# Layer 0 of a two-layer graph network: from one hand-written order of the products to three streams that a program clock merges, with the first pair also done by seven products

## The chip, the cores and the metric

The kernel runs on one core of one Trainium2 chip, in one launch. A core has TensorE (PE, matrix products into PSUM), ScalarE (ACT), VectorE (DVE), GpSimd (POOL) and SyncE (SP, which issues DMAs); PSUM, where products land, has eight banks of 128 x 512 float32. Everything here is float32. The metric is the device time of the core in microseconds, the median over runs: 2367.74 us before, from runs of 2363.7 to 2368.15 us.

## The reference, cut to what matters

`x` is 64 matrices of 256 x 256, `adj` one matrix of 256 x 256. Both layers are residual and begin with a layernorm and a relu.

```
G = adj * adj
h = relu(layernorm(x))
x = x + G relu(G relu(G h W1) W2) W3        # layer 0: W1 256x512, W2 512x1024, W3 1024x256
h = relu(layernorm(x))
U = eigenvectors of the normalised Laplacian of adj      # 256 x 256
x = x + U (relu(U^T h V1 + b1) V2 + b2)     # layer 1: V1 256x128, V2 128x256
```

Layer 0 needs only `G`, so it can run while the eigenvectors are found. Layer 1 needs `U`, except for its product `h V1`, which the kernel takes first, because `U^T h V1` is `U^T (h V1)`.

## The kernel before, in words

**Two kinds of work.** The class `Eigen` finds the eigenvectors by tridiagonalising and joining: a long chain of small DVE, POOL and ACT instructions with a few products (tiles `psA` to `psD`), one after the other. The class `Layers` works on 32 pairs `q` of input matrices. For each pair of layer 0 there are, in order: `begin` (load, layernorm and relu into `h0`, on ACT and POOL), `first` (G times h0, tile `y1`), `widened` (times W1, with a relu into `s1`), the spread (G times `s1`), the products with W2, `fourth` (with W3, tile `p3`), `last` (G times `p3`, added to `x1` on DVE and stored), `norm1` (layernorm of the new rows on ACT and POOL), `turn_rows` (PE transposes) and `for_layer1` (times V1, tile `hw`, stored).

**By seven.** For pairs from `SEVEN_FROM` = 1 on, the W2 product is made of seven half-sized products in place of eight. That needs sums of blocks of W2 (`fold_weights`: eight DVE subtractions and additions of 128 x 512, six into the tile `sums` and two in place), sums of blocks of its right-hand side (`spread_by_seven`: `forms` 0 to 2 are copied from PSUM, `forms` 3 to 5 are a copy of the negated block `forms` 6, and one DMA from POOL adds 0 to 2 onto 3 to 5), and a sum at the end (`add`, twice a pair, once for each half `jj`: a POOL DMA adds three blocks from `parts` onto `s2`). After each `add`, `rectify` applies the relu on ACT, and `fourth` can read that half. Pair 0 goes by eight (`third`, with the tile `y2`).

**Who sets the order.** The program writes out PE's and ACT's instruction order itself. A clock in the program, the class `Pace` (line 160), estimates when each instruction could start. The eigen chain calls `chain`: before it hands out an instruction of its own, `run` hands out those instructions of the streams that start earlier by the clock's estimate. `run` looks only at the head of each stream. DVE, POOL and SP get their order from the framework (the `manual_schedule` in `tile_kernel` names PE and ACT only), but each engine executes its own queue strictly in order.

**Two streams.** `streams` (line 1902) makes two: `products` (line 1905), which holds all PE work of layer 0 with the ACT copies that empty its PSUM banks, in one fixed order, and `rows`, which holds both norms, `begin(q + 2)` ahead of `norm1(q)`. Pair by pair the order in `products` is:

```
W2 of q (with last(q-1) between its first products), first(q+1), widened(q+1),
rectify half 0, turn_rows(q-1), spread part 1 of q+1, rectify half 1,
fourth of q, part 1, for_layer1(q-1), load of x1,
then the other spread parts of q+1 in turn with the other parts of fourth of q
```

**PSUM.** Layer 0 has four banks. `bank` gives them out in rotation, except those that are `held` over several products. Layer 1 has four more.

**The end.** When the chain has U, `go_on` hands out another 3.5 us of PE work, a flag is read by every engine (`mend`), and layer 1 runs as a further stream. The last pair's `turn_rows` waits for `due`, which is set there.

## Time and profile before

| what | value |
|---|---|
| median of three runs | 2367.74 us |
| the profiled execution, its own time | 2369.36 us |
| its span, first to last instruction | 2367.6 us |
| PE busy | 2290.2 us (97%) |
| PE weight loads busy | 1854.7 us (78%) |
| DVE, ACT, POOL busy | 2005.0, 1183.8, 698.7 us |
| PE idle from 100 to 1300 us, and from 1300 to 2150 us | 23.9 us, 22.9 us |
| flag of the eigen chain written | 2173.8 us |
| first product of layer 1 | 2181.0 us |

In the profile a PE row's time covers a run of products of one kind; two records stand for one float32 product of 256 columns. A product's record lasts beyond the time at which the next can start, so the pace of a run is read from one row's start to the next row's start. `bank<-L_gnn_W,y` is `widened`, `bank<-gt,s` the spread, `bank<-forms,...` the W2 products, `bank<-L_gnn_W,s` the products with W3, `bank<-p,gt` is `last`, `bank<-eye,x` is `turn_rows`, `bank<-L_gnn_W,x` is `for_layer1`, and `bank<-hw,u` the first product of layer 1. In square brackets stands how long the engine sat idle just before, and what ended that. All instructions carry line 208, where `issue` calls them.

### The profile page before, as it was taken

The page shows a single profiled execution, that of the slowest core. Times are in us where ns is not written, and L with a number is a line of the kernel's source. Part 1 is how long each engine was busy: PE and PEld are TensorE (multiplying, and loading weights), DVE is VectorE, ACT ScalarE, POOL GpSimd, SP SyncE. Part 2 cuts the span into 40 slices and gives each one's busy share as a digit, 9 for nine tenths or more (in the row PEclk, how much of TensorE's full clock was granted, in tenths as well). Part 3 has the DMA queues.
Part 4 walks back from the last instruction along what each step waited for, and adds up shares of the span by engine and source line. Part 5 has one row for each costly group of instructions (what it writes and reads, how often), then busy time and mean ns, then how long its engine had stood idle before and what let it go on. Part 6 is the DMA issues. An engine that isn't in the chain of part 4 may idle for free. (4 is left out here: it accounts for less than half of the span.)

```text
span 2367.6 us, 40804 instructions
## 1 busy us (share of the span) xinstructions
PE 2290.2 (97%) x10652; PEld 1854.7 (78%) x10652; DVE 2005.0 (85%) x12072; ACT 1183.8 (50%) x2951; POOL 698.7 (30%) x1946
## 2 busy tenths in 40 slices
PE   7999999999999999999999899999999999999999
PEld 4687878787777877787888788777778777887888
DVE  7999999999999999999999899999877687882343
ACT  4455554555555555555555345555554455543322
POOL 3444544445554222222222001111111111111443
PEclk9999999999999999999999999999999999999999
DMA  4022222122222222222222222322322222223675
GB/s 134 23 70 61 65 57 70 51 69 63 59 59 62 72 56 61 69 67 59 72 63 60 58 63 72 72 72 59 72 63 63 59 58 72 54 63 103 217 251 203
DMA packets 91359, 183.26 MB, mean 77 GB/s; under 512 B 8432, under 2 KB 61808, under 8 KB 91120
## 3 DMA queue, kind: packets, MB, share of 16 engines
q0 software_dynamic: 13392, 73.14, 15.6%
q1 hardware_dynamic: 77728, 107.45, 13.4%
q8 instruction: 86, 1.41, 0.2%
q14 instruction: 153, 1.25, 0.2%
HBM read 65.48 MB, written 41.94 MB: 45 GB/s over the span
## 5 line engine op out<-in xcount | busy, mean ns | idle before, releaser
L208 PE MATMUL bank<-forms,L_gnn_W 128*128 128x256 f32 (+2 forms) x2102 | 490.7, 382 | 9.2 <-DVE x L208 6.1
L208 PE MATMUL bank<-L_gnn_W,s 128*128 128x256 f32 x2086 | 476.0, 378 | 4.8 <-ACT s L208 4.7
L208 PEld LDWEIGHTS bank<-forms,L_gnn_W 128*128 128x128 f32 x2102 | 390.6, 191 | 73.3 <-issue 11.7
L208 PEld LDWEIGHTS bank<-L_gnn_W,s 128*128 128x128 f32 x2086 | 391.7, 192 | 57.3 <-ACT s L208 5.7
L208 ACT ACTIVATE s<-bank 128x512 f32<-128x512 f32 (+1 forms) x485 | 278.7, 579 | 174.3 <-PE bank L208 173.3
L208 PE MATMUL bank<-forms,sums 128*128 128x256 f32 (+1 forms) x1512 | 347.0, 377 | 0.0
L208 PEld LDWEIGHTS bank<-forms,sums 128*128 128x128 f32 x1512 | 283.3, 191 | 53.4 <-issue 15.5
L208 PE MATMUL bank<-gt,s 128*128 128x256 f32 (+1 forms) x1036 | 246.3, 377 | 1.1 <-ACT s L208 1.1
L208 PE MATMUL bank<-L_gnn_W,y 128*128 128x512 f32 (+3 forms) x538 | 230.8, 572 | 1.1 <-ACT y L208 1.1
L208 ACT ACTIVATE forms<-bank 128x512 f32<-128x512 f32 x217 | 128.9, 594 | 180.9 <-PE bank L208 180.7
L208 PEld LDWEIGHTS bank<-gt,s 128*128 128x128 f32 x1036 | 188.9, 190 | 24.8 <-ACT s L208 2.6
L208 POOL COPY m<-xr 128x1 f32<-128x1 f32 x254 | 59.9, 236 | 418.1 <-DVE xr L208 418.0
L208 PEld LDWEIGHTS bank<-L_gnn_W,y 128*128 128x128 f32 x538 | 98.7, 190 | 98.2 <-issue 87.3
L208 ACT ACTIVATE junk<-xr 128x254 f32<-128x254 f32 (+63 forms) x127 | 46.0, 362 | 200.5 <-DVE xr L208 200.4
L208 ACT ACTIVATE junk<-x 128x256 f32<-128x256 f32 x256 | 105.8, 413 | 71.9 <-issue 44.0
L208 DVE SCALAR_TENSOR_TENSOR A<-xr,wc,A 128x255 f32<-128x255 f32 (+63 forms) x381 | 139.2, 368 | 0.0
L208 DVE SCALAR_TENSOR_TENSOR A<-wr,q,A 128x255 f32<-128x255 f32 (+63 forms) x381 | 138.0, 365 | 0.0
L208 ACT ACTIVATE junk<-x,nm 128x256 f32<-128x256 f32 x256 | 128.7, 503 | 4.0
L208 PE MATMUL bank<-p,gt 128*128 128x512 f32 (+2 forms) x272 | 122.8, 567 | 0.0
L208 PE MATMUL bank<-gt,h 128*128 128x256 f32 (+1 forms) x520 | 119.1, 379 | 0.1
L208 DVE SCALAR_TENSOR_TENSOR r<-A,xr 128x255 f32<-128x255 f32 (+63 forms) x381 | 117.8, 309 | 0.2
L208 PE MATMUL psB<-ident,ac 128*128 128x128 f32 x381 | 84.7, 277 | 27.2 <-DVE z L208 15.0
(614 smaller groups left out, 4639.5 us busy)
## 6 DMA issues: line engine op xcount, KB each, us to landing
x<-in_x_dram SPq DMA_DIRECT2D x128, 256.0 KB, 3.0
x<-x SPq DMA_DIRECT2D x64, 512.0 KB, 3.5
forms<-forms POOLq DMA_DIRECT2D x31, 768.0 KB, 5.8
s<-s POOLq DMA_DIRECT2D x31, 768.0 KB, 5.9
s<-forms POOLq DMA_DIRECT2D x31, 768.0 KB, 5.8
hw<-hw SPq DMA_DIRECT2D x64, 256.0 KB, 3.1
out_dram<-out SPq DMA_DIRECT2D x64, 256.0 KB, 2.2
L_gnn_W<-in_L_gnn_W_dram SPq DMA_DIRECT2D x1, 2048.0 KB, 11.2
```

What stands on the lines that cost most here:

```text
L208: return op.call(*op.args, **op.kwargs)
```

## The change

- `products` is replaced by three streams that the clock merges: `narrow` (first, widened and spread of the next pair), `wide` (fold_weights, W2, rectify, fourth, last) and `turned` (turn_rows, for_layer1, load of x1). What orders them against each other are sets that they fill: `added` opens `widened` once the first `add` of the pair before has been handed out, `tripled` opens the spread once all its W2 products have, `formed` opens the W2 products, and `loaded` opens `last`.
- `rows` is split into one stream for each norm. `due` is gone.
- All pairs go by seven; `third` by eight, `y2`, `first_pair`, `spread_of` and `spread_in_turn` are gone. `fold_weights` is the first thing in `wide`.
- The blocks that the second `add` reads are now `forms` 3 to 5 in place of 0 to 2, and the four spread blocks follow one another in one bank.
- The four banks are four fixed tiles. `take` waits in the program for one that has been given back, and picks the one that the clock says is free first.
- The clock keeps the source of a DMA as being read until the DMA lands (4 or 6 us in its estimate), and no longer only for the time of its issue.

```diff
@@ class Pace
+    def free_at(self, t):
+        name, _, _ = span(t)
+        return max((x[2] for x in (*self.written.get(name, ()), *self.read.get(name, ()))), default=0.0)
@@ issue
-            self.read[name] = [*self.read[name][-15:], (lo, hi, start + busy, engine)]
+            self.read[name] = [*self.read[name][-15:], (lo, hi, start + (until if "dma" in op.name else busy), engine)]
@@ class Layers
-        self.parts = [self.s1.rearrange("p m b f -> p (m b) f")[:, 1:4], forms[:, 0:3]]
+        self.parts = [self.s1.rearrange("p m b f -> p (m b) f")[:, 1:4], forms[:, 3:6]]
-        self.banks, self.held = list(range(4)), {}
+        self.free_banks = [self.ps.tile([P, 512], F32, name=f"bank{i}") for i in range(4)]
+    def take(self):
+        yield lambda: len(self.free_banks) > 0
+        ps = min(self.free_banks, key=self.pace.free_at)
+        self.free_banks = [x for x in self.free_banks if x is not ps]
         return ps
+    def give(self, ps):
+        self.free_banks.append(ps)
     def streams(self):
-        return Stream(self.products()), Stream(self.rows())
+        return [Stream(x) for x in (self.narrow(), self.turned(), self.wide(), self.rows(), self.new_rows())]
+    def narrow(self):
+        for q in range(PAIRS):
+            yield from self.first(q)
+            yield lambda: q == 0 or q - 1 in self.added
+            for b in range(2):
+                yield from self.widened(b)
+            yield lambda: q == 0 or q - 1 in self.tripled
+            yield from self.spread()
+            self.formed.add(q)
+    def wide(self):
+        yield from self.fold_weights()
+        for q in range(PAIRS):
+            last = self.last(q - 1) if q > 0 else iter(())
+            yield lambda: q in self.formed
+            for part in self.third(q):
+                if part is None:
+                    yield from next(last, ())
+                else:
+                    yield part
+            self.tripled.add(q)
+            yield from self.fourth()
+        for part in self.last(PAIRS - 1):
+            yield from part
+    def turned(self):
+        for q in range(PAIRS + 1):
+            if q > 0:
+                yield lambda: q - 1 in self.h1
+                yield from self.turn_rows()
+                yield from self.for_layer1(q - 1)
+            if q < PAIRS:
+                for i in range(2):
+                    yield self.nc.sync.dma_start(out=self.x1[:, i], in_=self.view(self.ap["x"], q)[:, i])
+                self.loaded.add(q)
@@ third (was third_by_seven)
         yield from part("z", 0, 4, 2)
         yield self.add(0)
+        self.added.add(q)
@@ fourth
+        for jj in range(2):
+            yield from self.rectify(jj)
             for m in range(H):
-                yield from part(m, 0, at)
+                yield from part(m, 0, range(4 * jj, 4 * jj + 4))
+        for m in range(H):
             yield from part(m, 1, range(8))
             yield self.nc.scalar.copy(self.p3[:, m, :], banks[m])
-            self.free(banks[m])
+            self.give(banks[m])
```

## The prediction

> **What bounds the kernel.** I read the page first, then PE's waits in two stretches, then PE's timeline at a wait, and last the stretch in which the eigen chain ends.
>
> ```profile
> PE 2290.2 (97%) x10652; PEld 1854.7 (78%) x10652; DVE 2005.0 (85%) x12072; ACT 1183.8 (50%) x2951; POOL 698.7 (30%) x1946
> ```
>
> PE is busy for 2290.2 of 2367.6 us. PE's timeline in the middle of a pair says whether that is real work:
>
> ```profile
> 1628.31 7.03 PE L208 MATMUL bank<-L_gnn_W,y 128*128 128x512 f32 x16
> 1635.17 1.04 PE L208 MATMUL bank<-eye,x 128*128 128x128 f32 x8
> 1636.05 1.89 PE L208 MATMUL bank<-gt,s 128*128 128x256 f32 x8
> ```
>
> Start to start, 16 records of 512 columns take 6.86 us (0.429 each) and 8 of 256 take 1.73 (0.216 each), without a hole. So PE bounds the kernel, and all that another order can win is PE's idle time, 77.4 us. Of this 11.8 us (two waits, 4.6 and 7.2) are the start, where no product can run yet. The next answers, PE's waits from 100 to 1300 us and from 1300 to 2150 us, give most of the rest.
>
> ```profile
> PE psB L208 <- DVE z L208: 13.2, 17, 1.9
> PE psB L208 <- DVE xr L208: 9.0, 11, 1.7
> PE psB L208 <- DVE ac L208: 1.2, 2, 1.0
> ...
> PE bank L208 <- DVE x L208: 6.1, 5, 3.6
> PE bank L208 <- ACT s L208: 4.7, 2, 3.8
> ...
> PE bank L208 <- ACT forms L208: 3.2, 3, 1.1
> PE bank L208 <- ACT x L208: 1.3, 1, 1.3
> ```
>
> In the first stretch (23.4 us) PE waits only in front of the chain's transposes `psB`. That looks like the chain's fault, but the timeline of PE, and of ACT beside it, shows what lies ahead of such a wait:
>
> ```profile
> 766.90 1.04 PE L208 MATMUL bank<-eye,x 128*128 128x128 f32 x8
> 769.67 0.29 PE L208 MATMUL psB<-ident,ac 128*128 128x128 f32 x1 [1.73 <-DVE xr L208]
> ...
> 769.91 1.89 PE L208 MATMUL bank<-gt,s 128*128 128x256 f32 x8
> ...
> 769.23 1.56 ACT L208 ACTIVATE s<-s 128x1024 f32<-128x1024 f32 x2
> 770.70 0.57 ACT L208 COPY x<-bank 128x512 f32<-128x512 f32 x1
> ```
>
> The spread product at 769.91 needs only `s1`, which was ready, yet it stands behind `psB`. In the single stream it follows the ACT work of `rectify` and `turn_rows`, which a busy ACT reaches only at 769.23. The head of the stream waited for ACT, so the clock had no PE work to put ahead of `psB`. About one wait a pair is of this kind. Where PE had work the wait is shorter:
>
> ```profile
> 677.09 1.03 PE L208 MATMUL bank<-forms,L_gnn_W 128*128 128x256 f32 x4
> 678.78 0.40 PE L208 MATMUL psB<-ident,ac 128*128 128x128 f32 x2 [0.66 <-DVE z L208]
> ```
>
> The end of the chain, again PE's timeline: the last flag product of the chain is at 2173.26, and layer 0 still has 46 records with W3 and 8 of `last` after it, 9.9 + 3.4 us, then 2.6 us of transposes and V1 products. Layer 1 takes 165 us of PE after that.
>
> ```profile
> 2173.26 0.28 PE L208 MATMUL psC<-bad,ones 128*128 128x1 f32 x2
> 2173.40 4.56 PE L208 MATMUL bank<-L_gnn_W,s 128*128 128x256 f32 x20
> ...
> 2194.39 3.02 PE L208 MATMUL bank<-ut,s 128*128 128x256 f32 x8 [2.80 <-ACT s L208]
> ```
>
> **The change, part by part.** The sum is made against the profiled execution, 2369.36 us (span 2367.6 and 1.8 around it), which is 1.6 us above the median of the runs, 2367.74.
>
> *Pair 0 by seven.* Removed are 64 records of 512 columns, 64 x 0.429 = 27.5 us, and 16 short ACT copies. Added are 112 records of 256, 112 x 0.216 = 24.2, with 14 copies, two `rectify` (1.6 us each), one triple copy (1.48) and three POOL DMAs (issue 0.9 to 1.0 us each, 5.8 to landing) on queues that are idle there for most of the time. **-3.3 us.** The three DMAs lie behind the first six W2 products (10.3 us); without that cover each would cost its 5.8.
>
> *Three streams.* A head that waits for ACT no longer holds the PE work of the others. From 100 to 1300 us some 18 pairs pass (61 us of PE work each and the chain's own). Where the head was stuck a wait was 1.7; where PE had work it was 0.66, because the chain itself is late there: POOL's norm (1.0 us for the power alone) stands ahead of the chain's POOL work, and that stays. Bounds: 0 (all waits are the chain's) and 23.4. I take 18 x (1.2 - 0.65) = **-10 us**.
>
> *Banks by the clock, and other work beside a late bank.* From 1300 to 2150 us PE waits 15.3 us for banks or their readers. Those behind `DVE x` (6.1) are banks that an add on DVE still reads; the clock can now choose another bank, if it knows of the lateness, which it does only as far as its estimate of DVE goes. Those behind ACT stay where ACT itself is blocked by a late norm. Two gaps above 3.5 us cost more than themselves. The one of 3.61 us, at 1878.49, is followed by eight records in 3.78 us, which take 1.89 elsewhere. Bounds 0 and 15.3 + 2 x 1.9 = 19; I take the `DVE x` share with its slow records, **-7 us**.
>
> The Trainium skill ("TensorE: Matmul & The Clock Gate", Part 1) has a rule for this: after an idle window of about 3.4 us the clock falls to half and needs as long to come back. It speaks against the change at the start. There the new order puts both halves of `first` ahead of `widened`, and the second half's rows are ready only at 22.4 us, so PE would idle from 18.4. By the rule that costs one more cold start, an estimate of 1.7 us; by the trace, where eight records after the 7.2 us gap took 3.52 us for 1.89, 1.6.
>
> *The start.* `fold_weights` moves from beside pair 0 to the head of `wide`. Its eight DVE instructions (0.68 each, 5.4 us) were in the trace from 19.3 to 31.3 and at 69.9, partly in holes of the chain. The framework orders DVE, so they may now stand together in front of the chain's DVE work, and they need W2 (issued from 3.3 us on in a group of five, 11.2 to landing): if DVE reaches them earlier, it stops, and the chain, POOL, ACT's chain work and PE's `psB` behind it stop too. Bounds: 0, and 8 (from DVE's hole at 5.4 us to 15 is 9.6, less the hole of 3.3, and 1.6 for a cold clock). The spread waits for the evacuation of one bank three times (1.1 us each), with nothing beside it for pair 0. Against that the old start had 2.3 us of waits of its own. I take **+2**, near the low end, since DVE ran the first of them at 19.29 with no wait.
>
> *What loses its cover.* Before, each `add` (trigger 0.3 us after ACT's last copy, 5.8 to landing) had `first` and `widened` behind it, 16 records of each, 3.5 + 6.9 us of PE. Now `first` runs earlier; `widened` opens at the first `add`, so part of it still lies there, then the spread (32 records, 6.9 us) and `for_layer1`. The triggers are not always prompt. Here, in POOL's and ACT's timelines, the add's last source was copied by 1562.22, its DMA began 3.64 us later because POOL sat behind a chain instruction, and `rectify` came at 1576.50:
>
> ```profile
> 1561.62 0.60 ACT L208 ACTIVATE forms<-bank 128x512 f32<-128x512 f32 x1 [0.85 <-PE bank L208]
> 1565.35 0.23 POOL L208 COPY zn<-q 128x32 f32<-128x32 f32 x1 [7.22 <-DVE q L208]
> 1565.86 0.86 POOL L208 DMA_DIRECT2D s<-forms  x1 [0.28 <-ACT y L208]
> ```
>
> That left 4.8 us after the landing at 1571.7. An ACT that reaches `rectify` too early stops in order, and with it every evacuation and the chain's own ACT work; then PE. Bounds: 0, and 31 pairs x 1.1 us = 34 (0.3 + 5.8 + 1.58 of `rectify` is 7.7, 0.8 more than the spread's 6.9, and 0.3 for late triggers). I take **+8**, a quarter us a pair, because `wide` has the lower priority and reaches `rectify` after the others' work.
>
> *Split norms, `due`, x1 loads.* The same instructions, and 64 x1 loads on SP with their wait for `for_layer1`'s reads as before. Loads for the other norm behind them in SP's queue had a whole pair of slack; if it were gone, each would cost its 3.0 us. **0**, hidden by that slack. DMA sources held longer in the clock: no instruction, 0.
>
> *The end.* With some 10 us less before the flag, less of the 16 us of layer 0 is left over. That is already in the sum, as PE work is only moved. The hole from 2173.4 to 2181.0 (flag, fetch) must still be filled by about 7.5 us of it. Gained is part of the wait for ACT at 2194.39 (2.8). Bounds: -4, and +7.5 if nothing is left to fill the hole. **-2**.
>
> Sum: -3.3 - 10 - 7 + 2 + 8 + 0 - 2 = -12.3. From 2369.4 that gives 2357 for the profiled kind of execution, and from the median **2355.5**.
>
> The skill's front page ("Trainium Kernel Development and Optimization", Performance Expectations) calls busy time of matmuls a bad measure and weight loads a good one. By that, 78% loaded would leave an estimated 513 us open. By the rows above 77 us are open, since records follow each other at 0.216 with the load of 0.19 inside. I go by the rows.
>
> **Rivals.**
>
> *The old order was as good* (0.17). For it: from 1628 to 1684 us PE runs without a wait. Then the waits at `psB` are all the chain's, new small ones eat the rest, and only pair 0 counts: 2363 to 2372, say 2365. Against it: the spread product at 769.91 that stood ready behind the wait.
>
> *The `add` loses its cover, slower* (0.26). One mechanism: ACT in order behind `rectify` and behind the first relu into `s1`, which must wait for the first `add`'s read, because the POOL trigger or the landing is later than the clock's 6 us. At 34 us the sum is -12.3 - 8 + 34 = +13.7, so 2381; 2372 to 2400. It decides from (12.3 + 8)/31 = 0.65 us a pair on. For it: triggers late by up to 3.6 us. Against it: the margin of 4.8 us even there, and the priority of the other streams.
>
> *The streams hang on the banks* (inside the first rival). W2 holds up to four banks at its eighth product, and then three streams are one again; the change would not do what it says. 2365.
>
> **How the numbers follow.** The forecast, 2343 to 2363, gets 0.57. The measurement can tell 0.2%, 4.7 us: faster below 2363.0, slower above 2372.5. Faster 0.57, same 0.17, slower 0.26. The range from 2342 to 2388 leaves out one in ten on the side of the slow rival's tail and a little below.
>
> **What would show it.** PE busy some 3 us lower, and the rows of 512 columns for W2 gone. No PE wait of more than 1 us behind an `eye` row from 100 to 1300 us, and `psB` waits near 13 us in place of 23.4. `DVE x` under 2 us. PE waits behind `ACT s` or gaps in the spread would show the slow rival, with ACT waiting for the DMAs `s<-s` and `s<-forms`, which it now does once. A stop of DVE near 5 to 15 us with `sums` next would show the start's worst case. The prediction is wrong if the chain, and no longer PE, sets the time at which the flag is written, or if the new waits at `rectify` pass 0.65 us a pair.

## The result, and the profile after

The changed kernel takes 2387.65 us (median; 2384.98 to 2388.84), the kernel before on the same chips 2367.94: a ratio of 1.0085, 95% interval 1.0068 to 1.0103. It is slower by 20 us. The forecast was 2355.5; the sign was wrong, though 2388 was the upper end of the range. The profiled execution took 2384.98 us, its span is 2383.2 (2367.6 before), so the profiled spans differ by 15.6 us where the medians differ by 19.7.

First the page: PE's line, and the costliest group (busy time, mean ns | idle time before it, and what ended most of it).

```profile
PE 2298.8 (96%) x10700; PEld 1852.8 (78%) x10700; DVE 2008.6 (84%) x12072; ACT 1208.2 (51%) x2954; POOL 693.7 (29%) x1949
...
L211 PE MATMUL bank<-L_gnn_W,s 128*128 128x256 f32 (+1 forms) x2078 | 488.1, 378 | 15.8 <-ACT s L211 15.4
```

PE looks as busy as before, and by its work it is lighter: with each record counted at its pace (0.216 us per 256 columns, 0.429 per 512) the work is 2248.3 us, 3.3 less than before, as forecast for pair 0. The idle time in front of the W3 products has grown: 15.8 us, 4.8 before. Next, PE's waits of the changed kernel from 100 to 1300 us (what for; us in total, times, longest).

```profile
PE psB L211 <- DVE z L211: 10.8, 17, 1.3
PE bank L211 <- ACT s L211: 8.4, 12, 1.5
PE bank L211 <- ACT x L211: 5.6, 10, 1.0
PE psB L211 <- DVE ac L211: 0.8, 1, 0.8
...
PE psB L211 <- DVE xr L211: 0.5, 1, 0.5
```

And the same from 1300 to 2150 us.

```profile
PE bank L211 <- ACT s L211: 6.5, 9, 1.6
PE bank L211 <- ACT x L211: 5.3, 14, 0.7
PE bank L211 <- DVE x L211: 3.1, 2, 2.3
```

The waits in front of `psB` fell from 23.4 to 12.1 us, and those behind `DVE x` from 6.1 to 3.1: the first as the prediction had it (near 13), the second half-way to it (under 2), and yet the kernel is slower. In their place are many short waits of PE behind ACT. Over the whole run PE waited 14.8 us behind ACT's `s`, `x`, `forms`, `h` and `y` before, and 45.8 after. One of them, in PE's timeline (start, us, what, idle time before it and its releaser):

```profile
236.56 1.03 PE L211 MATMUL bank<-L_gnn_W,s 128*128 128x256 f32 x4
239.05 0.70 PE L211 MATMUL bank<-L_gnn_W,s 128*128 128x256 f32 x2 [1.46 <-ACT s L211]
239.58 1.46 PE L211 MATMUL bank<-gt,s 128*128 128x256 f32 x6
```

and beside it in ACT's timeline:

```profile
237.09 0.39 ACT L211 ACTIVATE junk<-xr 128x222 f32<-128x222 f32 x1 [3.19 <-DVE xr L211]
...
237.47 0.58 ACT L211 ACTIVATE forms<-bank 128x512 f32<-128x512 f32 x1
237.95 1.56 ACT L211 ACTIVATE s<-s 128x1024 f32<-128x1024 f32 x2
```

ACT stands idle for 3.19 us because its next instruction in order is the chain's own (`junk<-xr`), and DVE hasn't made `xr` yet. Behind it stand the evacuation, whose product ended at 236.72, and `rectify` (`s<-s`), whose `add` had landed at 234.19. So `rectify` comes 3.8 us after its data, most of which ACT stood idle, and PE, which was given the W3 product for the moment when `rectify` was estimated to end, waits 1.46 us. What follows on PE, the chain's next `psB` included, waits with it.

The start of the changed kernel, in DVE's timeline:

```profile
17.36 1.29 DVE L211 TENSOR_TENSOR sums<-L_gnn_W 128x512 f32<-128x512 f32 x2
18.56 2.49 DVE L211 TENSOR_TENSOR sums<-L_gnn_W,sums 128x512 f32<-128x512 f32 x4
20.97 1.28 DVE L211 TENSOR_TENSOR L_gnn_W<-L_gnn_W 128x512 f32<-128x512 f32 x2
```

and in PE's timeline:

```profile
23.71 0.66 PE L211 MATMUL psB<-ident,xc 128*128 128x128 f32 x2 [4.62 <-DVE xc L211]
...
39.63 3.28 PE L211 MATMUL bank<-gt,s 128*128 128x256 f32 x8 [3.64 <-ACT forms L211]
```

The eight folds stand in one block of 4.9 us in front of the chain's DVE work, and the chain's first transpose waits 4.62 us for it. Later the spread waits 3.64 us for one evacuation, and the eight records behind that wait take 3.28 us, 1.89 elsewhere (the granted clock is 0.50 from 40.3 to 43.5 us).

The clearest view is a table of when the chain got where. "Step n" is the start of the n-th group of transposes `psB<-ident,ac` in PE's timeline, counted from 0 (two records a group, one from step 127 on).

| us from the start of the span | before | after | difference |
|---|---|---|---|
| step 0 | 23.36 | 28.35 | +5.0 |
| step 20 | 156.06 | 163.71 | +7.7 |
| step 100 | 618.78 | 641.10 | +22.3 |
| step 250 | 1286.42 | 1311.24 | +24.8 |
| flag written | 2173.77 | 2194.75 | +21.0 |
| first `hw,u` product of layer 1 | 2181.01 | 2202.32 | +21.3 |
| end of the span | 2367.59 | 2383.21 | +15.6 |

So the loss is 5.0 us in front of the chain's first step, 17.3 in its first 100 steps, 2.5 in the next 150; after them 3.8 us come back up to the flag and 5.7 in layer 1, which has less of layer 0 beside it (32 records with W3 come after the flag product, 46 before).

To see what the chain's steps wait for, I followed the trace back from step 250 to step 0, stretch by stretch, by the rule of the page's chain (to what released an instruction, or else to the one before it on its engine). Before, of 1263 us of path 816 are layer 0's instructions on PE, 23 layer 0's on ACT and 11 on POOL; after, of 1283 us, 736 on PE, 106 on ACT and 32 on POOL. So in both kernels the chain spends most of this stretch behind layer 0's products in PE's order, and the path now leads through ACT far more often, above all through the norms' instructions, the relus into `s1` and `rectify`.

### The profile page after: what moved, and what is told of

The parts are those of the page before. It is cut to its first block, busy times and chain, and to the rows that moved or that the text cites. A ratio compares the mean times of both kernels' runs of the same rounds, so it can differ in the third digit from the quotient of the medians.

```text
span 2383.2 us, 40954 instructions
## 1 busy us (share of the span) xinstructions
PE 2298.8 (96%) x10700; PEld 1852.8 (78%) x10700; DVE 2008.6 (84%) x12072; ACT 1208.2 (51%) x2954; POOL 693.7 (29%) x1949
## 5 line engine op out<-in xcount | busy, mean ns | idle before, releaser
L211 PE MATMUL bank<-L_gnn_W,s 128*128 128x256 f32 (+1 forms) x2078 | 488.1, 378 | 15.8 <-ACT s L211 15.4
L211 PE MATMUL bank<-forms,L_gnn_W 128*128 128x256 f32 (+1 forms) x2094 | 495.8, 375 | 4.2 <-DVE x L211 3.1
L211 PEld LDWEIGHTS bank<-forms,L_gnn_W 128*128 128x128 f32 x2094 | 383.6, 190 | 86.3 <-issue 34.7
L211 ACT ACTIVATE s<-bank 128x512 f32<-128x512 f32 x480 | 281.7, 590 | 249.4 <-PE bank L211 229.3
L211 PE MATMUL bank<-forms,sums 128*128 128x256 f32 (+1 forms) x1552 | 362.1, 378 | 1.1 <-ACT s L211 1.1
L211 PEld LDWEIGHTS bank<-forms,sums 128*128 128x128 f32 x1552 | 291.1, 191 | 75.7 <-issue 35.2
L211 PE MATMUL bank<-L_gnn_W,y 128*128 128x512 f32 (+3 forms) x536 | 253.2, 576 | 1.1 <-ACT s L211 0.5
L211 PE MATMUL bank<-gt,h 128*128 128x256 f32 (+1 forms) x518 | 126.0, 382 | 6.6 <-ACT h L211 6.6
L211 ACT ACTIVATE junk<-x 128x256 f32<-128x256 f32 x256 | 106.0, 414 | 42.9 <-issue 23.2
L211 PE MATMUL bank<-p,gt 128*128 128x512 f32 (+3 forms) x278 | 123.4, 559 | 0.0
L211 PEld LDWEIGHTS bank<-gt,h 128*128 128x128 f32 x518 | 97.9, 193 | 20.4 <-ACT h L211 7.8
## 6 DMA issues: line engine op xcount, KB each, us to landing
L_gnn_W<-in_L_gnn_W_dram SPq DMA_DIRECT2D x1, 2048.0 KB, 10.7
```

What stands on the lines that cost most here:

```text
L211: return op.call(*op.args, **op.kwargs)
```

## The experiments

The theories, by the letters that the expectations use:

- **P**: PE's work and idle time set the time, as the prediction assumed.
- **K**: the eigen chain sets the time at which the flag is written. A PE wait in front of layer 0's instruction holds up the chain behind it; a wait in front of `psB` costs nothing more.
- **A**: the new waits come from instructions put on an engine just in time, with no slack for an ACT that is late in order.
- **B**: the `add` DMAs have lost their cover (the prediction's slow rival).
- **C**, later **S**: the start. **R**: ACT takes the norms' relus too early, before POOL has made their `shift`.

**e1: the folds later.** In `wide`:

```
     def wide(self):
+        yield lambda: 0 in self.begun
         yield from self.fold_weights()
```

> The same kernel as after, but the stream of the wide products folds W2 only once both products of the first pair's first stage are issued (self.begun holds pair 0), not as its very first instructions. Theory C (the start: eight instructions of DVE in one block from 17.4 to 22.2 us delay the chain, and all behind it carries the delay to the end): the chain's first psB transpose comes 4.6 us earlier, the first W2 product of pair 0 at about 43 in place of 49.8 us, and the time falls by 5 to 8 us, to 2380-2383. Theory A (the loss is made later, by streams that get PE the moment the clock thinks their data ready): the start's part alone, which PE's lost time in the first 100 us puts at 8.2, may fall, at most 8; if the chain's delay of 5 us is made up anyway by the time that the flag is written, 0 to 3, 2385-2388.

Measured: 2381.07 us, ratio 1.0064 [1.0043, 1.0085], 6.6 less than after. Step 0 comes at 21.65, step 250 at 1305.64, flag at 2189.87: the 5.6 us gained by step 250 are kept nearly in full to the end. So what delays the chain at its start is paid at the end, as C and K have it. Steps 20 to 250 take 1147.7 us, 1147.5 in after: the larger part of the loss is untouched.

**e2: a margin for PE.** In `run`, with SLACK at 1.0 and at 0 in layer 1:

```
-                    start = max(self.ready(op), self.clock[op.engine])
+                    slack = self.SLACK if op.engine == "PE" else 0.0
+                    start = max(self.ready(op) + slack, self.clock[op.engine])
```

> As after, but where the clock chooses the next instruction among the streams, an instruction for PE counts as ready only 1.0 us after the clock's estimate of its data (the issue itself and the chain's own instructions are as they were; layer 1 has no such margin). Theory A (no slack: each real lateness of ACT, in order behind the chain's own ACT work, becomes a wait of PE): the new waits in front of eye, L_gnn_W,s, L_gnn_W,x and gt,s rows (35 to 41 us in all) fall by half or more, at the cost of some us of psB waits again: 15 to 25 us faster than after, 2363-2373. Theory B (the add on POOL's DMA has lost its cover; the data come several us late): a margin of 1 us doesn't reach it; within 4 us of after, 2384-2392. Theory C (the start): no change, 2385-2390.

Measured: 2387.76 us, ratio 1.0093 [1.0074, 1.0113]. The time is that of after, so A's number is wrong. Its mechanism is in the trace, though: PE's waits of the kernel with the margin, from 100 to 1300 us.

```profile
PE psB L212 <- DVE z L212: 5.4, 11, 1.0
PE psB L212 <- DVE xr L212: 2.3, 5, 0.7
PE bank L212 <- ACT s L212: 1.6, 4, 0.6
PE bank L212 <- ACT x L212: 1.5, 3, 0.7
PE bank L212 <- ACT forms L212: 1.3, 2, 1.0
```

PE's waits there fell from 27.4 us to 12.1, those behind ACT from 14.7 to 4.4. Step 250 comes 10.8 us earlier than in after and pair 19's W2 products 31.5 us earlier (1325.7 against 1357.2), and the time didn't move: from step 250 to the flag it took 895.4 us (883.5 in after). 30 us of PE's time won by 1300 us were worth nothing at 2385. P can't explain that, and neither can K alone, for which the 10.8 us at step 250 should have lasted; why the later stretch got longer stays open.

**e3, e4: the streams undone, and their order of asking.** e3 replaces the three streams by one in the order of before; e4 swaps two of them.

```
-        return [Stream(x) for x in (self.narrow(), self.turned(), self.wide(), self.rows(), self.new_rows())]
+        return [Stream(x) for x in (self.one(), self.rows(), self.new_rows())]
...
+    def one(self):
+        yield from self.fold_weights()
+        yield from self.first(0)
...
+            yield from self.rectify(0)
+            forms = self.spread_steps() if more else iter(())
+            if q > 0:
+                yield lambda: q - 1 in self.h1
+                yield from self.turn_rows()
+            yield from next(forms, ())
+            yield from self.rectify(1)
...
```

> As after (pair 0 by seven, the folds at the head, PSUM banks chosen by the clock, norms in two streams), but the products of layer 0 again in one stream in the order of before. Theories A and B (the three streams cost more than they bring): the new waits in front of eye, L_gnn_W,s, L_gnn_W,x and gt,s go (some 35 us), the waits at psB between 100 and 1300 us come back (15 us) and the end loses its 6.5 us: 2387.7 - 35 + 15 + 6 = 2374, at most the start's 5 to 8 us above before: 2368-2378. Theory C (only the start and its delay count, the streams are neutral): 2384-2390. Whether banks known to the clock are worth their 7 us shows in the stretch from 1300 to 2150 us: PE's wait for banks behind DVE x there at 3 us or less, 6.1 before.

> As after, but at equal times the stream of the W2 and W3 products is asked before that of the turned rows (it was behind it). Theory A, where the waits in front of turn_rows (eye) and for_layer1 (L_gnn_W,x), some 27 us, come from turning rows and copies being put on PE the moment they are estimated ready: they get slack whenever W2 products stand ready, and fall by about half, while the fourth product's waits (19 us) stay or grow by some 4: 2374-2382. If the waits come from ACT being blocked in order whatever is asked first, no change: 2384-2391. Theory B: no change.

Measured: e3 2376.56 us, ratio 1.0044 [1.0030, 1.0059]; e4 2408.38, ratio 1.0179 [1.0157, 1.0200]. The three streams cost 11.1 us against one with the same start. In e3 the waits at `psB` are back (25.1 us from 100 to 1300), those behind ACT are gone, and steps 20 to 250 take 1132.6 us (1130.4 before). e4 is a miss: asking `turned` last, which was to give it slack, made PE's waits behind `ACT s` there grow from 8.4 to 13.6 us.

**e5: less work on PE.** The kernel before, which here leaves out the second of the two products that each `widened` block adds up:

```
-            yield from self.products_of(ps, [(self.y1[:, c, at : at + P], w1[:, c, :]) for c in range(2)])
+            yield from self.products_of(ps, [(self.y1[:, c, at : at + P], w1[:, c, :]) for c in range(1)])
```

> The kernel before, with part of the computation left out: each widened product adds only the first of its two matmuls of 512 columns, so PE has 128 x 0.429 = 55 us less work of layer 0, spread evenly over the pairs; ACT's, DVE's and the chain's instructions are all there. Theory P (PE's work sets the time, as the prediction has it): the time falls by about 50 us, to 2313-2323. Theory K (the eigen chain sets the time at which the flag is written, and layer 0 only has to fit between its steps): the flag product stays at 2174 us, give or take 6, PE gets 50 us more of idle time, above all in front of psB, and the time falls only by what layer 0 had left after the flag, 5 to 15 us: 2351-2363.

Measured: 2353.02 us, ratio 0.9944 [0.9924, 0.9964]: 12.7 us for 55 us of PE's work. The time lies in K's range (5 to 15 less) and far from P's (about 50). Its page:

```profile
PE 2193.1 (93%) x10366; PEld 1806.9 (77%) x10366; DVE 2006.0 (85%) x12072; ACT 1179.6 (50%) x2951; POOL 697.0 (30%) x1946
```

its timeline of PE at the flag:

```profile
2168.89 0.28 PE L208 MATMUL psC<-bad,ones 128*128 128x1 f32 x2
2176.30 2.05 PE L208 MATMUL bank<-hw,u 128*128 128x256 f32 x4 [7.14 <-DMA hw<-hw]
```

and its longest wait of PE from 1300 us to the end:

```profile
PE psB L208 <- DVE m L208: 34.8, 1, 34.8
```

The flag product moved from 2173.26 to 2168.89 only. PE ran out of layer 0's work and stood 34.8 us in one wait for the chain and 7.14 for the fetch. Of the 17.6 us between the two profiled spans 4.7 lie ahead of layer 1's first product; the other 12.9 are layer 1, which takes 173.7 us from there to the end (186.6 before) when nothing of layer 0 is left beside it. So in the kernel before it was not the amount of PE's work that set the flag's time, but the chain. That is the chain as it runs between layer 0's products, and not untouched by them: steps 20 to 250 took 1143.4 us in e5 (1130.4 before), with no more than 0.6 us of PE's idle time in front of layer 0's products, and only the stretch from step 250 to the flag got shorter (870.7 us, 887.3 before). Why those steps got longer is open, and no run shows how long the chain takes with nothing beside it.

**e6: pair 0 by seven alone**, in the kernel before:

```
-SEVEN_FROM = 1
+SEVEN_FROM = 0
...
-            for half in range(2):
-                yield from self.spread_of(b, half)
+        for part in self.spread_by_seven():
+            yield from part
```

> The kernel before with one part of the change alone: pair 0 also by seven products, in the one stream; W2 is folded right before the first W2 product, after pair 0's spread, as the one stream has it. Theory P: PE's work falls by 3.3 us, and the time with it if the fold doesn't hold PE up, 2362-2366; if PE waits for the folds, 2366-2370. Theory K: what counts is when the chain makes its first steps. The folds come after the chain's first steps, so those stay where they were (first psB at about 18 and first step at 23.4 us) and the time stays within 3 us of before: 2363-2369.

Measured: 2366.32 us, ratio 1.0006 [0.9997, 1.0016]. Less PE work and no time won, as K has it, though 3.3 us is little above the noise and the ranges of P and K overlap here. Step 250 came at 1282.91.

**e7, e8: folds later and a margin during the chain's steps.** e1's and e2's edits with SLACK 2.0 (e7) or 1.5 (e8), and

```
     def tridiagonalize(self, a):
...
+        self.pace.SLACK = 0.0
         return drow, erow, us, gams
```

> As after, with two edits: W2 is folded once pair 0's first stage is issued (the edit that took 6 us off), and a stream's instruction for PE counts as ready 2.0 us after the clock's estimate of its data, while the chain makes its 254 steps only, not after. Theory K (a PE wait in front of a stream's instruction holds up the chain's instruction behind it in PE's order, and only that costs time; a wait in front of psB costs nothing): the waits in front of eye, L_gnn_W and gt,s rows from 100 to 1300 us fall from 29 us to under 8, the chain's step 250 comes at 1285-1296 us (1311 in after), the rest of the chain takes some 884 us as in after, and layer 1 190: 2360-2370. Theory P: a margin moves PE's lost time and doesn't shorten it, so only the fold counts: 2378-2385.

> As the one with a margin of 2.0 us, but 1.5 us. Theory K: the real lateness of ACT in the waits of after was 1.5 us at most, so 1.5 does what 2.0 does: within 4 us of it, 2360-2372. Theory P: 2378-2385.

Measured: e8 2375.08 us, ratio 1.0037 [1.0023, 1.0051]; e7 2405.86, ratio 1.0164 [1.0147, 1.0181]. In e8 steps 20 to 250 take 1132.1 us, as in the one stream: the margin takes the streams' cost out of them. The other traces agree. PE's idle time in front of layer 0's products between steps 20 and 250, and what these steps took, are 0.0 and 1130.4 us in before, 0.0 and 1132.6 in e3, 1.3 and 1132.1 in e8, 4.2 and 1138.7 in e2, 14.6 and 1147.5 in after, 19.8 and 1152.0 in e4, 23.2 and 1154.5 in e11 (below); in front of the chain's own `psB` and `psA` it is 19.9, 22.8, 12.3, 7.7, 10.7, 5.8 and 6.3 us in the same order, and the steps' time doesn't grow with it. This is K for the chain's steps; e7 (4.6 and 1142.3) and e5 lie above that line. But in e8 steps 0 to 20 take 145.3 (132.7 before). e7 is a plain miss of K's number: step 250 came at 1301.39, close to e8, but the stretch to the flag took 894.4 us and layer 1 204.8, with layer 0 not done by the flag: 26 records of W2 products were still to come after the flag product, none in before. There layer 0's work left over lengthens the end. That the rest takes some 884 and 190 us whatever came before was too simple.

**e9, e14: what is left without the streams.** e9 is e3 with the folds behind pair 0's spread; e14 also has the first pair's order of before:

```
     def one(self):
-        yield from self.fold_weights()
-        yield from self.first(0)
         for b in range(2):
+            yield from self.first_of(0, b)
+            if b:
+                self.begun.add(0)
             yield from self.widened(b)
         for part in self.spread_steps():
             yield from part
+        yield from self.fold_weights()
```

> The kernel of e3 (all of the change but the three streams of products) with W2 folded behind pair 0's spread, where the one stream of before would do it, in place of at the head. What is left of the change is pair 0 by seven, the banks chosen by the clock and the split norms. Theory K (only what holds the chain up counts): the chain's first step comes at 21 to 23 us, not 28.6, step 250 some 7 us earlier than in e3, at 1283-1286, and the time is that of before within 4 us: 2363-2370. The banks then bring nothing by themselves: PE's waits behind DVE x from 1300 to 2150 us stay at about 6 us, as in before. If the banks were worth the 7 us that the prediction gave them, 2356-2361.

> The kernel of e9 (the products in one stream, W2 folded behind pair 0's spread) with the start of before for the first pair. What is left of the change is pair 0 by seven, the banks known to the clock and the split norms. Theory S: step 20 at 153 us as in e6 and the time that of e6 and of before, 2363-2369; the banks known to the clock are worth nothing by themselves. If what e9 lost to e6 (8.5 us) lies in the banks, it stays at 2372-2377.

Measured: e9 2374.86 us, ratio 1.0033 [1.0021, 1.0045], outside K's 2363 to 2370; e14 2368.02, ratio 1.0005 [0.9995, 1.0014]. PE's timeline in e9:

```profile
20.84 2.93 PE L211 MATMUL bank<-gt,h 128*128 128x256 f32 x6 [3.54 <-ACT h L211]
...
25.27 6.08 PE L211 MATMUL bank<-L_gnn_W,y 128*128 128x512 f32 x12
33.50 0.54 PE L211 MATMUL psB<-ident,ac 128*128 128x128 f32 x2 [2.15 <-DVE xr L211]
```

and in e14:

```profile
18.03 2.84 PE L211 MATMUL bank<-L_gnn_W,y 128*128 128x512 f32 x6 [0.46 <-ACT y L211]
...
23.80 1.89 PE L211 MATMUL bank<-gt,h 128*128 128x256 f32 x8
```

With both halves' first products ahead, PE stands 3.54 us behind the second half's rows, and the six records after it take 2.93 us, 1.46 elsewhere; the granted clock is 0.50 from 20.0 to 26.7 us. Step 20 comes at 162.3 in e9 and 154.5 in e14; the times differ by 6.8 us. The Trainium skill ("TensorE: Matmul & The Clock Gate", Part 1) says that an idle window of about 3.4 us puts the clock at half; the trace agrees here (0.49 us a record behind 3.54 us of idle time; 0.24 in e14, without such a stand). e14 also settles the banks: with them known to the clock, and all else as before, PE's waits from 1300 to 2150 us still have the line

```profile
PE bank L211 <- DVE x L211: 7.0, 5, 3.6
```

(6.1, 5 times, 3.6 before). The shorter wait in after came with the streams, not with the banks. The traces of e6 and e14 show the same instructions in the same order on PE, ACT and POOL, so the split norms and the banks changed no order here.

**e10: later adds in the clock.**

```
-            self.busy, self.until = (1.0, 6.0) if self.engine == "POOL" else (0.1, 4.0)
+            self.busy, self.until = (1.0, 9.0) if self.engine == "POOL" else (0.1, 4.0)
```

> As after, but the clock counts 9.0 us in place of 6.0 from a POOL DMA's issue to its landing, so that rectify and the next pair's relu into s1 are put behind the adds with 3 us more. Theory B (the adds' DMAs land later than the clock believes, and ACT stops at rectify; this is the prediction's slow rival): PE's waits in front of L_gnn_W,s fall from 22 us to under 8, ACT's waits for the DMAs s<-s and s<-forms go, and the time falls by 10 us or more, to 2370-2378. Theory A (ACT stands in order behind the chain's own ACT instruction and the norms, not behind a DMA): the waits move but don't go, 2383-2392.

Measured: 2408.76 us, ratio 1.0177 [1.0160, 1.0194]. ACT's waits in after, over the whole run:

```profile
ACT h L211 <- POOL shift L211: 29.4, 18, 3.6
ACT s L211 <- DMA s<-s: 18.4, 9, 2.6
ACT x L211 <- POOL shift L211: 14.4, 19, 1.8
ACT s L211 <- DMA s<-forms: 12.3, 8, 2.7
```

and in e10:

```profile
ACT h L211 <- POOL shift L211: 19.9, 12, 4.6
ACT x L211 <- POOL shift L211: 19.8, 18, 6.7
...
ACT s L211 <- DMA s<-forms: 3.3, 1, 3.3
```

PE's two largest waits in e10, over the whole run:

```profile
PE bank L211 <- ACT s L211: 22.2, 27, 4.2
PE bank L211 <- ACT x L211: 16.2, 26, 4.6
```

The adds do land late in after: ACT waits 30.7 us for them, 3.6 before. 3 us more in the clock took that away, down to 3.3 us, and PE's waits behind `ACT s` stayed (20.6 in after, 22.2 here). So B has a true symptom, but the late adds aren't what PE's waits come from. The later `rectify` put layer 0 back instead: layer 1 took 198.1 us with the leftover, 180.9 in after.

**e11: the norms in one stream again.**

```
-        ... self.wide(), self.rows(), self.new_rows())]
+        ... self.wide(), self.rows())]
...
+            for p in [1, 2] if q == 0 else [q + 2]:
+                if p < PAIRS:
+                    yield lambda: p - 1 in self.begun
+                    yield from self.begin(p)
             yield lambda: q in self.new
             yield from self.norm1(q)
```

> As after, but the norms of layer 0's input and of the new rows in one stream, in the order of before. If two norm streams let ACT be taken by norms at the wrong time (ACT's norm instructions lie on the chain's path more often in after), the chain's first 100 steps get shorter and the time falls by 4 to 10 us, 2377-2384. If the norms in two streams are neutral, 2384-2391. If the three streams need a second norm stream, as turn_rows would otherwise wait for a norm behind the next pair's, slower than after: 2392-2405.

Measured: 2428.54 us, ratio 1.0267 [1.0250, 1.0284], 41 us above after and beyond the largest case expected. The three streams need the split norms; in the kernel with one stream of products both forms give the same order of instructions (e6 and e14).

**e12, e13, e15: start and margin put together.** e12 has the folds behind pair 0's spread and the margin of 1.5 us from pair 0's end on. e13 has the start of before and the folds of e1, e15 these and the margin.

```
         for q in range(PAIRS):
-            yield from self.first(q)
-            yield lambda: q == 0 or q - 1 in self.added
-            for b in range(2):
-                yield from self.widened(b)
+            if q == 0:
+                for b in range(2):
+                    yield from self.first_of(0, b)
+                    if b:
+                        self.begun.add(0)
+                    yield from self.widened(b)
+            else:
...
             yield from self.fourth()
+            if q == 0:
+                self.pace.SLACK = 1.5
```

> As after, with W2 folded behind pair 0's spread, and with the margin of 1.5 us for the streams' PE instructions from the end of pair 0's W3 products to the chain's last step (in e8 it stood from the start, and there the chain lost 12 us in its first 20 steps). Theory K with A: the first 20 steps take some 135 us as in e1, and steps 20 to 250 some 1132 us as in e8 (1147.5 in after), so step 250 comes at 1288-1293, the flag 885 us later at 2173-2179, layer 1 takes 181-187 as before: 2360-2368, level with before or a little faster. If the margin doesn't carry over, 2372-2380, as e8 and e1.

> As after, with the start of before for the first pair's products: each half's first product is followed by its widened products, not both halves' first products ahead of both widened; and W2 is folded once the second half's first product is issued. In e9 the new order alone put PE behind the second half's rows (3.5 us wait, then records at half pace to 34 us), with the chain behind it. Theory S (the start is worth more than the fold): the chain's step 20 comes at 152-155 us (157.9 in e1, 163.7 in after), and the time falls from e1's 2381 by 3 to 6 us, to 2374-2379. If the chain makes up that delay anyhow, 2379-2384. Both leave the just-in-time part of some 10 us against before.

> All of the change, with three edits: the start of before for the first pair (as e13), W2 folded once the second half's first product is issued, and the margin of 1.5 us for the streams' PE instructions from the end of pair 0 to the chain's last step. Theory K (the time is the chain's: its start, then its steps, then 884 us, then layer 1 in 181-187): step 20 at 152-156, steps 20 to 250 in 1132 as in e8 and e12, so step 250 at 1284-1288, and 2357-2365, 1 to 8 us faster than before. If the start's gain is lost again later, as e12, 2367-2373.

Measured: e12 2370.65 us, ratio 1.0015 [1.0005, 1.0024]; e13 2378.62, ratio 1.0045 [1.0030, 1.0061]; e15 2376.54, ratio 1.0041 [1.0027, 1.0055]. e12 is 2.6 us above K's range: steps 20 to 250 took 1133.0 us as expected, but steps 0 to 20 took 141.6 in place of 135. e13's time lies in S's range, e15's 11 us above K's, with steps 20 to 250 at 1140.1 us in place of 1132, and in both step 20 fails: it comes at 163.1 and 161.6, not at 152 to 156, although step 0 is early (23.3 and 21.0). The trace of e13 shows a place where three streams lose it. POOL's timeline:

```profile
35.10 0.37 POOL L211 COPY m<-xr 128x1 f32<-128x1 f32 x1 [3.07 <-DVE xr L211]
...
36.62 1.16 POOL L211 TENSOR_TENSOR scale<-v,rsqrt 128x4 f32<-128x4 f32 x1
37.85 0.27 POOL L211 TENSOR_TENSOR shift<-nm,scale 128x4 f32<-128x4 f32 x1
```

ACT's timeline:

```profile
38.16 1.58 ACT L211 ACTIVATE h<-x,shift,scale 128x256 f32<-128x256 f32 x3 [3.38 <-POOL shift L211]
...
40.53 0.57 ACT L211 ACTIVATE forms<-bank 128x512 f32<-128x512 f32 x1
```

and PE's timeline:

```profile
41.16 2.88 PE L211 MATMUL bank<-gt,s 128*128 128x256 f32 x8 [4.33 <-ACT forms L211]
```

POOL stands 3.07 us in order behind the chain's copy of `xr`; the next pair's norm behind it is late by about that; ACT has taken the relu that needs this norm and stands 3.38 us; pair 0's evacuation, whose data were ready, stands behind the relu; PE stands 4.33 us behind the evacuation, and the chain's next `psB` behind PE. One late value of the chain has gone through three queues and come back to the chain.

**e16, e17, e18: the relus too.** e16 is after with

```
+                    normed = op.engine == "ACT" and isinstance(op.kwargs.get("scale"), bass.AP)
-                    start = max(self.ready(op), self.clock[op.engine])
+                    start = max(self.ready(op) + (self.NORMED if normed else 0.0), self.clock[op.engine])
```

and NORMED at 2.0. e17 is e15 with this, e18 e17 with PE's margin at 1.0 us.

> As after, but where the clock chooses among the streams, the relu that ends a norm (on ACT, with scale and shift from POOL) counts as ready 2.0 us after the clock's estimate. In after ACT takes such a relu early and stands for 44 us in all, 37 times, behind POOL's shift, and everything behind it in ACT's order stands too (in the first pair's spread PE then waits 3.6 us for an evacuation). Theory R (that is where the late evacuations come from): ACT's waits for shift fall from 44 to under 15 us, PE's waits behind ACT from 39 to under 25, step 250 comes 8 us or more earlier, the time falls by 5 to 15 us, 2373-2383. Theory A in its wider form (any ACT instruction can be late, the chain's own above all, so taking one cause away lets the next one through): 2384-2391.

> The kernel of e15 (all of the change, the start of before, the fold later, PE's margin of 1.5 us from pair 0's end to the chain's last step) with the margin of 2.0 us for the norms' relus too, all the way. Theory R with K: the first pair's spread loses its wait of 4.2 us and the records at half pace behind it, so step 20 comes at 153-157 (161.6 in e15), steps 20 to 250 in 1132-1140, and the time is 2360-2370, level with before. If the waits only move to other places, 2371-2379.

> As e17 with PE's margin 1.0 in place of 1.5 us. If the margin's size matters little (e7 and e8 had step 250 within 1.5 us of each other), within 5 us of e17. A faster kernel than before, 2355-2363, would need step 250 at 1280-1286 as in before.

Measured: e16 2380.93 us, ratio 1.0054 [1.0039, 1.0068]; e17 2370.19, ratio 1.0011 [1.0002, 1.0020]; e18 2374.61, ratio 1.0028 [1.0017, 1.0039]. e16's time lies in R's range, but not by R's way. ACT's waits over the whole run:

```profile
ACT s L212 <- DMA s<-s: 21.6, 12, 3.1
ACT s L212 <- DMA s<-forms: 13.7, 7, 4.9
ACT h L212 <- POOL shift L212: 6.6, 5, 2.5
```

and the largest of PE's:

```profile
PE bank L212 <- ACT s L212: 25.0, 30, 2.5
```

ACT's waits for `shift` fell from 43.8 us to 7.1, as the edit must make them; PE's waits behind ACT's same five outputs stayed at 38.8 (45.8), and step 250 came at 1313.65, no earlier. The two profiled executions, 2383.44 and 2384.98 us, lie closer than the medians, so what took the 6.7 us between these stays open. Before, ACT already waited 39.2 us for `shift`, so these waits as such are not what the change brought. Taking one cause away let the next one through, which is A in its wider form. In e17 the path from step 0 to step 250 is again mostly PE's (of layer 0, 850 us on PE, 26 on ACT, 10 on POOL), and its time is the lowest with three streams (0.5 us under e12, within the noise): 0.1% slower than before, 0.2 us above the range expected, with step 20 at 159.7, not 153 to 157. Over the whole run PE still waits 33.2 us behind those outputs of ACT in e17, but only 2.6 between steps 20 and 250: it is there that such a wait costs. e18 stays within 5 us of it, as expected. None of these versions beats the kernel before.

## Why the prediction was wrong, point by point

The runs make a ladder from before to after, by medians:

| kernel | us | ratio to before |
|---|---|---|
| before, pair 0 by seven (e6) | 2366.32 | 1.0006 |
| and banks by the clock, split norms (e14) | 2368.02 | 1.0005 |
| and both first products of pair 0 ahead (e9) | 2374.86 | 1.0033 |
| and the folds at the head (e3) | 2376.56 | 1.0044 |
| and three streams (after) | 2387.65 | 1.0085 |

**The bound.** The step that failed first is "So PE bounds the kernel, and all that another order can win is PE's idle time". PE was 97% busy because the clock puts layer 0's instructions wherever the chain leaves room; it wasn't what set the end. e5 took 55 us of its work away for 12.7, and the flag product came 4.4 us earlier. The prediction named this as what would make it wrong ("if the chain, and no longer PE, sets the time at which the flag is written"), but as something that the change would bring; it had been so all along. Both readings that it weighed, 77 us open and 513 us open, ask how full PE is, and e5 shows that this was not the question.

**Pair 0 by seven, -3.3.** Right for PE's work (-3.3), worth nothing in time that e6 could tell from noise.

**Three streams, -10.** The waits at `psB` fell by 11.3 us, about as forecast. Such a wait is PE waiting for the chain. Filling it moves layer 0 forward, and that is worth only what layer 0 leaves over after the flag. The term should have been 0 in front of the flag; what it did bring is in layer 1 (180.9 us, 185.8 in e3).

**Banks by the clock, -7.** `DVE x` fell by 3.0 us in after, but not through the banks (e14: 7.0), and the time of e14 is that of before. The term is 0.

**The start, +2, bounds 0 and 8 with 1.6 for a cold clock.** In the one stream it measured +8.5 (e14 to e3: 6.8 for pair 0's order and 1.7, within the noise, for the folds); in three streams the folds alone measured 6.6 (e1). The mechanisms were both named, the block of folds and the cold clock behind the second half's rows; the value was taken at the wrong end, because the first fold had run without a wait before. That row said that W2 was there, not that the chain could spare DVE.

**What loses its cover, +8, bounds 0 and 34.** The size was wrong and the place half right. PE's waits behind ACT grew by 31 us, and the streams cost 11.1 us by the ladder; between steps 20 and 250, 14.6 us of waits in front of layer 0's products, 14.0 of them behind ACT, go with steps that take 14.9 us longer than in e3. They are ACT's order, as the rival had it, but not behind the adds: e10 took ACT's waits for the adds from 30.7 us to 3.3 and PE's waits stayed. In front of ACT stand the chain's own instruction, a norm's relu, or an add, whichever is late. Therefore the threshold of 0.65 us a pair, which was about `rectify` alone, was the wrong thing to watch.

**Norms, 0.** Neutral in one stream, but without the split the three streams would cost 41 us more (e11). The term 0 was right for this change and hid that the parts depend on each other.

**The end, -2.** Layer 1 took 5.7 us less from its first product on: the right direction, more than forecast. The wait for ACT that was to shrink (2.80 us) is still 2.37; what shrank is what layer 0 left over, though the flag came later and not earlier.

**The chances.** The slow side got 0.26. Of the slow rival, its time (2381, 2372 to 2400) is nearer than the forecast, and its rule of order (ACT in order passes lateness to PE) is what the traces show. The Trainium skill says it in one sentence ("PSUM — Partial Sum Buffer", Engine vs sequencer instructions): "ScalarE/VectorE/GpSimdE queues are strict FIFO", and matmuls start and complete in program order. The timelines at 237.09 and 35.10 us agree: 3.19 us of an idle ACT and 3.07 of an idle POOL, in front of work whose data came early in that time (`rectify`'s `add` at 234.19, the norm's last ACT instruction at 33.12). It is the rule that spoke against this change and that the prediction priced for one cause only.

**What stays open.** Why steps 0 to 20 take up to 145 us with three streams, most with a margin (132 to 133 in before, e6 and e14), beyond the one stand shown for e13. And why the stretch after step 250 takes 884 us in some orders and 895 in others (e2, e4, e7), with layer 1 up to 204.8: e10 (889.8) shows one long wait of PE there, 4.57 us behind an ACT that waited 6.74 for POOL, but no run took that stretch apart. Nor does any run show why e5's steps took longer with less work.

## What to carry to other kernels

When a serial chain and filler work share in-order engines, take away a known amount of the filler's work first: if the time hardly moves, the busy engine is not the bound, and waits in front of the chain's own instructions are not there to be won. Then price a new order by what it puts directly in front of the chain's instructions on every engine, and how late that can be. A plan that gives an engine an instruction at the very moment its data are estimated needs slack of the size of the real lateness, here 1 to 1.5 us; with it the three streams came level with the one order (e12, e17), not ahead of it.

## What was not expected of the hardware

A cold clock can last longer than the wait that caused it. In e15 PE stood 4.18 us for an evacuation at 38.69 us; the eight records behind it took 3.78 us (1.89 elsewhere), the next six, behind a gap of 0.69, 2.50 us (1.46 elsewhere), the eight from 47.59 us on 2.23, and only those from 50.09 us on took the usual 1.89. The granted clock is 0.50 from 38.1 to 48.2 us and 1.00 on both sides: some 10 us of half clock after the stand, with short gaps between. In the same stretch of e14 the longest stand was 1.83 us and eight records took 1.99 us.
